# A message-passing layer on one core: pair work begins two slots later, ScalarE writes three seeds of the tail, GpSimd normalises one unit of the end

## The chip, the cores and the metric

The kernel runs on one core of a Trainium2 chip. The metric is the device time of one execution in microseconds; lower is better. The profile names the engines PE (TensorE matmul), PEld (TensorE weight load), DVE (VectorE), ACT (ScalarE), POOL (GpSimd) and SP (SyncE, which here only issues DMAs). Each engine works through its own instructions strictly in the order in which the program lists them, and waits on semaphores for the others.

## The reference

There are 6250 nodes and 100000 edges with 128 features each. Edges are sorted by `dst`; `src` is random.

```python
edge_index = jnp.stack([src, dst])          # row = src, col = dst
msg_in = concatenate([x[row], x[col], edge_attr], axis=-1)      # 100000 x 384
h = msg_in @ W + b                                               # W is 384 x 128
h = (h - mean(h)) * rsqrt(var(h) + 1e-5) * gamma + beta          # per edge
msg = relu(h)
out = segment_sum(msg, row, num_segments=6250)
x = x + out
result = (x - mean(x)) / sqrt(var(x) + 1e-5)                     # per node
```

## The kernel before

**Slots and scatters.** The edges are cut into 782 tiles of 128 edges, and four tiles make a slot, so the main loop runs over slots q = 0 to 195. In slot q, TensorE forms the part of `h` that comes from the edge features and from `x[dst]` (`edges`: eight matmul records of L619 and four of L623), ScalarE copies it from PSUM into a row buffer `hs` (`evict`: L633, and every third slot a `fill`, L568), and GpSimd scatters the rows, tile by tile, to an array in HBM that is ordered by source node (`scatters`: L650, one indirect DMA a tile). The row buffer is a ring of nine slots in three groups of three: `fill` waits until the three slots that last used its group have been scattered. From slot 13 to slot 194 each scatter of slot q-1 is also tied to a matmul of slot q (`TIE`, `add_manual_dep`), so GpSimd cannot run ahead of TensorE.

**Splits, pairs and steps.** The tiles form six splits of 168, 168, 168, 120, 80 and 78 tiles, each with its own array `sorted`. When a split has been scattered, its rows are read back in "pairs" (two blocks of 125 source nodes, `hl`, loaded by SP at L725, with four buffers). A pair goes through 14 to 16 steps (the list `FLOW`): VectorE builds one-hot matrices (`ones`, L748), TensorE transposes them (`turn`, L760), ScalarE copies the result (`turned`, L764) and writes the pair's rows into a PSUM bank (`seed`, L770), TensorE adds the source nodes' projections (`pick`, L787), ScalarE takes squares (`square`, L796) and roots, VectorE scales and clips (`scale`, L811), TensorE sums by node (`sums`, L820), VectorE adds to the accumulator (`add`, L826). A new pair enters every four steps. A pair of the first three splits has eight row blocks, of the fourth six; of the fifth split eight double pairs come first, then nine of four row blocks.

`work(n)` issues n steps; how many have to be issued by slot q is a straight line between the points of the list `due`, of which each is (slot, steps):

```python
n = steps_due(q + 1) - n_steps
work(min(n, 1))
evict(s, q)
...
work(n - 1)
if TIE[0] < q < TIE[1]:
    scatters(len(waiting) - PT, True)
```

In slot q these lines follow `edge_loads` and `edge_window` (up to four slots ahead, on SP), `edge_hot(q + 2)` (L607, VectorE) and `edges(s, q)`. The load of a pair is issued six steps before its `ones`. SP's queue holds edge loads (L141, L581, L593), clears of the next split's array (L236) and pair loads (L725) in one order; the first pair load of a split waits there until the split's last scatter has landed. The numbers of `due` before are (45, 0), (87, 100), (129, 200), (159, 300), (181, 400), (190, 432), (197, 468): the first three splits' pairs begin three slots behind the last slot of their split.

**The tail.** The pairs of the last split are the 14 units 0 to 13 (sizes 1, eleven times 2, 1, 1 pairs; four row blocks a pair). `tail(i)` issues for unit i: `root` and `scale` of unit i-1 (DVE, L898 and L905), `pick(0)` and `pick(1)` (PE), `ones` of unit i+2 (DVE, L854), `var` of unit i-3 (ACT, L947 and L950), `turn` of unit i+1 (PE, L864), `square` (ACT, L890 and L893), `turned` of unit i+1 (ACT, L867), `sums` and `add` of unit i-1 (PE L919, DVE L925), `begin` of unit i-1 (POOL, L932), `stats` of unit i-2 (DVE, L937), `norm` of unit i-3 (DVE, L956 and L958) and its `end`: two POOL instructions (L964, L965) and the store (SP, L970). In `pick` TensorE writes the rows into the bank by a product with the identity (L873), two records a time, and then adds twelve products (L879). The banks named `sel` are three, those named `hp` two; pair p of the last split takes `hp` where p mod 4 is 3.

The last four units are written out; a is the fourth last and b, c, d the last three. They end so:

```python
for u in (b, d, c):
    u.norm()
    u.end(True)
```

With `end(True)` VectorE normalises the unit's rows block by block (L968; four blocks for b, two for d and for c), and SP stores them (L970). The stores stand in SP's queue in the order b, d, c.

Of the kernel before, what the change touches and what calls it, by code (L numbers as in the profile page):

```python
# [17 lines left out]
D = 128  # L18
# [4 lines left out]
TILES = 782  # L23
LAST = E - (TILES - 1) * P
NB, BN = 50, 125
RUN = 8
NPAD = 6400
PT = 4
# [9 lines left out]
SPLITS = [(168, 4, 320, [12, 24, 44, 44, 44]),  # L38
          (168, 4, 320, [42, 42, 42, 42]),
          (168, 4, 320, [42, 42, 42, 42]),  # L40
          (120, 3, 192, [40, 40, 40]),
          (80, 2, 128, [40, 40]),
          (78, 2, 128, [39, 39])]
# [15 lines left out]
def first_tiles():  # L59
    out = [0]  # L60
    for n, _, _, _ in SPLITS:
        out.append(out[-1] + n)
    assert out[-1] == TILES
    return out
# [20 lines left out]
def fast_path(ctx, tc, io, bad_d, found):  # L85
# [3 lines left out]
    nc = tc.nc  # L89
    first_tile = first_tiles()  # L90
# [8 lines left out]
    def pe(i, cost=1):  # L99
        done.append((i.ins, cost))  # L100
        return i
# [76 lines left out]
    ident = const.tile([P, P], F32, name="ident")  # L178
# [551 lines left out]
    class Pairs:  # L730
# [35 lines left out]
        def seed(self, g):  # L766

            j0, m = self.groups[g]
            self.sel[g] = psum.tile([P, PT, P], F32, name="sel", bufs=BANKS["sel"])
            nc.scalar.copy(self.sel[g][:, :m, :], self.hl[:, j0:j0 + m, 0:D])  # L770

        def pick(self, g):


            j0, m = self.groups[g]
            if g in self.sel:
                sel = self.sel[g]
            else:
                name = "hp" if (g + self.p * len(self.groups)) % 2 else "sel"
                sel = psum.tile([P, PT, P], F32, name=name, bufs=BANKS[name])  # L780
                nc.tensor.matmul(sel[:, :m, :], ident, self.hl[:, j0:j0 + m, 0:D], start=True,
                                 stop=False, skip_group_check=True)
                self.sel[g] = sel
            for j in range(m):
                b = self.block(j0 + j)
                for i in range(3):
                    pe(nc.tensor.matmul(sel[:, j, :], self.ohn[:, j0 + j, :],  # L787
                                        xa[:, b, i * D:(i + 1) * D], start=False,
                                        stop=j == m - 1 and i == 2, skip_group_check=True))
# [45 lines left out]
    class Unit:  # L835
# [30 lines left out]
        def turned(self):  # L866
            nc.scalar.copy(self.ohn[:, :self.k, :], self.tr[:, :self.k, :])  # L867

        def pick(self, g):
            j0, m = g * self.kp, self.kp  # L870
            name = "hp" if (self.p0 + g) % 4 == 3 else "sel"
            sel = psum.tile([P, PT, P], F32, name=name, bufs=BANKS[name])
            nc.tensor.matmul(sel[:, :m, :], ident, self.hl[:, j0:j0 + m, 0:D], start=True,  # L873
                             stop=False, skip_group_check=True)
            self.sel[g] = sel
            for j in range(m):
                b = 2 * (self.p0 + g) + j % 2
                for i in range(3):
                    nc.tensor.matmul(sel[:, j, :], self.ohn[:, j0 + j, :],  # L879
                                     xa[:, b, i * D:(i + 1) * D], start=False,  # L880
                                     stop=j == m - 1 and i == 2, skip_group_check=True)
# [91 lines left out]
    n_split = len(SPLITS)  # L973
# [95 lines left out]
    TWINS = 8  # L1069
    pairs, first_item = [], []  # L1070
# [50 lines left out]
            n_steps += 1  # L1121

    LEAD, ENDQ, ENDS = 6, 1, 0
    LAG = 3
    MOST = 6.6

    due = []
    for s in range(1, n_split):
        q = first_tile[s] // PT + LAG
        if due:  # L1130
            q = max(q, due[-1][0] + int(NB * SPLITS[s - 2][1] / MOST))
        due.append((q, 4 * first_item[s - 1]))
    q, at0 = due[-1]
    due.append((q + int(4 * TWINS * SPLITS[-2][1] / MOST), at0 + 4 * TWINS))
    due.append((-(-TILES // PT) + ENDQ, len(pairs) * 4 + ENDS))

    def steps_due(q):
# [16 lines left out]
    for s, (n_tiles, _, _, _) in enumerate(SPLITS):  # L1154
        p0, p1 = first_tile[s] // PT, -(-first_tile[s + 1] // PT)
        slots = p1 - p0
        for i in range(slots):
            q = p0 + i
# [45 lines left out]
    def at(i):  # L1204
        return 0 <= i < n

    def tail(i):
        u = lambda j: units[i + j]
        if at(i - 1):
            u(-1).root()  # L1210
            u(-1).scale(0)
        if at(i):
            u(0).pick(0)
        if at(i - 1) and u(-1).n > 1:
            u(-1).scale(1)
        if at(i):
            if u(0).n > 1:
                u(0).pick(1)
        if at(i + 2):
            u(2).ones()  # L1220
            if at(i + 4):
                u(4).load()
        if at(i - 3):
            u(-3).var()
        if at(i + 1):
            u(1).turn()
        if at(i):
            u(0).square()
        if at(i + 1):
            u(1).turned()  # L1230
        if at(i - 1):
            for g in range(u(-1).n):
                u(-1).sums(g)
                u(-1).add(g)
            u(-1).begin(nc.gpsimd)
        if at(i - 2):
            u(-2).stats()
        if at(i - 3):
            u(-3).norm()
            u(-3).end()  # L1240
# [23 lines left out]
    for i in range(1, n - 1):  # L1264
        tail(i)
# [4 lines left out]
    a, b, c, d = units[-4:]  # L1270
# [21 lines left out]
    c.var()  # L1292
    for u in (b, d, c):
        u.norm()
        u.end(True)
    order.close()


@with_exitstack
def gnn_resnorm_kernel(ctx, tc, io):  # L1300
    nc = tc.nc
    keep = ctx.enter_context(tc.tile_pool(name="keep", bufs=1))
    bad_t = keep.tile([1, 1], I32, name="bad_t")
    with ExitStack() as inner:
        found = []
        fast_path(inner, tc, io, bad_t, found)
    with tc.If(found[0] > 0, preferred_fallthrough_block=True, label="general"):
        with ExitStack() as inner:
            general_path(inner, tc, io)
# [233 lines left out]
```

## Time and profile before

| what | value |
|---|---|
| median of 3 runs | 1121.99 us (1118.9 to 1122.06) |
| profiled execution | 1117.85 us |
| its span, first to last instruction | 1115.9 us |
| mean granted TensorE clock | 0.906 |
| busy: PE, DVE, ACT, POOL | 870.6, 846.7, 751.9, 795.9 us |

The profile's rows come from the profiled execution. Its span is 1.95 us shorter than its time. In a timeline row the first number is the start from the span's beginning, the second the duration, the bracket the idle time of the engine just before and what ended it.

### The profile page before, as it was taken

To read this page: it belongs to the slowest core of one execution; us is meant where nothing else is said; L and a number is where in the kernel's file an instruction comes from. 1 tells how busy PE (TensorE), PEld (TensorE's weight loads), DVE (VectorE), ACT (ScalarE), POOL (GpSimd) and SP (SyncE) were. 2 spreads that over 40 slices of the span, in tenths; PEclk is the share of its full clock that TensorE was granted. 3 is DMA by queue.
4 is the path that set the end of the run, shared out by engine and by line. 5 is a ranking of instruction groups with operands and counts; after the bars stand their busy time and mean duration, and the time that the engine had idled before them with its cause. 6 is when DMAs were issued, how large, how long until landed. Compare 5 with 4: busy or idle time off the path is not lost. (4 is left out here: it accounts for less than half of the span.)

```text
span 1115.9 us, 27253 instructions
## 1 busy us (share of the span) xinstructions
PE 870.6 (78%) x8886; PEld 805.4 (72%) x8886; DVE 846.7 (76%) x2368; ACT 751.9 (67%) x2980; POOL 795.9 (71%) x830
## 2 busy tenths in 40 slices
PE   6748755456878888598968678988989899987994
PEld 4647645456867887587868668888878788886773
DVE  8784556628769586688877668889898988877897
ACT  4324422126666667577777657898888899987895
POOL 2777777777777777777777777777777767774254
PEclk7879878668989788898989897999999999999998
DMA  7899999458777763877867648787778767844341
GB/s 216 262 267 272 283 311 284 150 182 286 230 228 253 234 205 126 270 231 245 274 223 242 186 134 281 244 253 241 230 245 259 226 209 241 262 136 141 105 134 61
DMA packets 128049, 247.19 MB, mean 222 GB/s; under 512 B 47005, under 2 KB 61231, under 8 KB 127897
## 3 DMA queue, kind: packets, MB, share of 16 engines
q1 hardware_dynamic: 101924, 191.92, 56.9%
q0 software_dynamic: 25104, 53.05, 13.2%
q8 instruction: 71, 1.16, 0.5%
q14 instruction: 80, 0.66, 0.2%
q10 hardware_dynamic: 870, 0.40, 0.1%
HBM read 155.49 MB, written 89.80 MB: 220 GB/s over the span
## 5 line engine op out<-in xcount | busy, mean ns | idle before, releaser
L650 POOL DMA_INDIRECT sorted<-hs,place_i x782 | 757.5, 969 | 249.8 <-issue 100.9
L787 PE MATMUL sel<-xa,ohn 128*128 128x128 bf16 x2550 | 188.9, 226 | 83.7 <-ACT sel L770 82.0
L619 PEld LDWEIGHTS hp<-w,eT 128*128 128x128 f32 x1564 | 216.4, 212 | 48.7 <-issue 30.2
L820 PE MATMUL pa<-msg,ohe 128*128 128x130 f32 x1700 | 236.6, 292 | 17.1 <-DVE acc L826 8.6
L619 PE MATMUL hp<-w,eT 128*128 128x128 f32 x1564 | 237.7, 300 | 14.1 <-ACT hs L633 14.1
L811 DVE SCALAR_TENSOR_TENSOR msg<-sel,rstd,cut 128x128 f32<-128x128 f32 x850 | 240.6, 345 | 8.0
L796 ACT ACTIVATE sq<-sel 128x128 f32<-128x128 f32 x850 | 223.7, 282 | 23.1 <-PE sel L787 23.1
L787 PEld LDWEIGHTS <-ohn 128*128 128x128 bf16 x2550 | 165.7, 101 | 94.3 <-issue 80.2
L820 PEld LDWEIGHTS pa<-msg,ohe 128*128 128x128 f32 x1700 | 213.9, 201 | 23.2 <-DVE acc L826 10.4
L796 ACT ACTIVATION_READ_ACCUMULATOR sq<-sel 128x1 f32 x850 | 180.9, 213 | 0.0
L748 DVE TENSOR_TENSOR ohe<-hl,beside 128x1024 f32<-128x1024 f32 (+2 forms) x117 | 130.2, 1113 | 57.2 <-DMA hl<-sorted 41.1
L633 ACT COPY hs<-hp 128x512 f32<-128x512 f32 x196 | 113.2, 579 | 59.1 <-PE hp L623 56.7
L770 ACT COPY sel<-hl 128x512 f32<-128x512 f32 (+1 forms) x225 | 128.1, 569 | 33.0 <-DVE msg L811 32.7
L764 ACT COPY ohn<-tr 128x1024 bf16<-128x1024 bf16 (+2 forms) x117 | 107.7, 921 | 5.3 <-PE tr L760 5.3
L607 DVE TENSOR_SCALAR ohd<-db,part_w 128x512 bf16<-128x512 bf16 x192 | 70.4, 367 | 51.7 <-DMA db<-drel_d 48.6
L568 ACT COPY hs<-sloc 128x12 f32<-128x12 f32 x66 | 14.1, 213 | 132.9 <-DMA sorted<-hs,place_i 131.1
L826 DVE TENSOR_TENSOR acc<-acc,pa 128x260 f32<-128x260 f32 x125 | 52.3, 418 | 57.6 <-PE pa L820 56.7
L760 PE MATMUL tr<-ident_h,ohe 128*128 128x128 bf16 x850 | 70.5, 227 | 26.8 <-DVE ohe L748 14.9
L623 PE MATMUL hp<-win,ohd 126*128 126x128 bf16 x782 | 80.8, 228 | 2.3 <-DMA win<-xb_d 2.3
L805 DVE RECIPROCAL rstd<-std 128x4 f32<-128x4 f32 (+1 forms) x225 | 38.1, 169 | 57.7 <-ACT std L799 56.0
L760 PEld LDWEIGHTS <-ohe 128*128 128x128 bf16 x850 | 55.6, 102 | 28.0 <-DVE ohe L748 16.1
L799 ACT ACTIVATE std<-ss,eps 128x4 f32<-128x4 f32 (+1 forms) x225 | 66.9, 297 | 7.3
(198 smaller groups left out, 1039.3 us busy)
## 6 DMA issues: line engine op xcount, KB each, us to landing
eT<-in_eT SPq DMA_DIRECT2D x96, 512.0 KB
hl<-sorted SPq DMA_DIRECT2D x75, 528.0 KB
db<-drel_d SPq DMA_DIRECT2D x96, 256.0 KB
sorted<-empty SPq DMA_DIRECT2D x100, 198.0 KB
hl<-sorted SPq DMA_DIRECT2D x50, 264.0 KB
sorted<-hs,place_i POOLq DMA_INDIRECT x782
hl<-sorted SPq DMA_DIRECT2D x25, 396.0 KB
sorted<-empty SPq DMA_DIRECT2D x50, 132.0 KB
```

Of the source, the lines that this page charges most:

```text
L619: pe(nc.tensor.matmul(hp[:, j, :], eT[:, at], w[:, 2, :], start=j == 0, stop=False, skip_group_check=True), 4)
L623: pe(nc.tensor.matmul(hp[:, j, :], oh[:3 * WN, at], win[:3 * WN, :], start=False, stop=j == m - 1, skip_group_check=True))
L633: nc.scalar.copy(hs[:, :m, 0:D], hp[:, :m, :])
L650: i = nc.gpsimd.indirect_dma_start(out=sorted_d[s][:, :], out_offset=bass.IndirectOffsetOnAxis(ap=place_i[:parts, t:t + 1], axis=0), in_=h ...
L748: nc.vector.tensor_tensor(self.ohe[:, :k, :], self.hl[:, :k, D:D + 1].to_broadcast([P, k, P]), row_bc(iota_p, k), op=ALU.is_equal)
L760: pe(nc.tensor.transpose(tr[:, j, :], half[:, j0 + j, 1::2], ident_h))
L764: nc.scalar.copy(self.ohn[:, :self.k, :], self.tr[:, :self.k, :])
L770: nc.scalar.copy(self.sel[g][:, :m, :], self.hl[:, j0:j0 + m, 0:D])
L787: pe(nc.tensor.matmul(sel[:, j, :], self.ohn[:, j0 + j, :], xa[:, b, i * D:(i + 1) * D], start=False, stop=j == m - 1 and i == 2, skip_gro ...
L796: nc.scalar.activation(sq[:, j, :], self.sel[g][:, j, :], AF.Square, accum_out=ss[:, j:j + 1])
L811: nc.vector.scalar_tensor_tensor(self.msg[:, j0 + j, 0:D], self.sel[g][:, j, :], rstd[:, j:j + 1], cut, op0=ALU.mult, op1=ALU.max)
L820: pe(nc.tensor.matmul(self.pa[:, h, :], self.ohe[:, i * k + j, :], self.msg[:, i * k + j, :], start=(j == h), stop=(j == k - 2 + h)), 4)
```

## The change

- `LAG` goes from 3 to 5 and `MOST` is gone. The points of `due` become (47, 0), (89, 100), (131, 200), (161, 300), (181, 400), (190, 432), (197, 468): the first four are two slots later, the last three as before. From slot 45 to slot 177 one to nine fewer steps have been issued than before by the end of the same slot (seven at slot 131, eight at slot 161); between slots 161 and 181 the steps come at 5.0 a slot, where they came at 4.55 from 159 to 181.
- In the tail's units 1 to 3 the rows of the second pair are written into their bank by ScalarE (a copy) and not by TensorE.
- Unit b is ended by POOL's two instructions, not by VectorE's four. `norm` of b stays on VectorE, and the three stores keep their order.

```diff
-        def pick(self, g):
+        def seed(self, g, engine):
             j0, m = g * self.kp, self.kp
             name = "hp" if (self.p0 + g) % 4 == 3 else "sel"
             sel = psum.tile([P, PT, P], F32, name=name, bufs=BANKS[name])
-            nc.tensor.matmul(sel[:, :m, :], ident, self.hl[:, j0:j0 + m, 0:D], start=True,
-                             stop=False, skip_group_check=True)
+            if engine is nc.scalar:
+                nc.scalar.copy(sel[:, :m, :], self.hl[:, j0:j0 + m, 0:D])
+            else:
+                nc.tensor.matmul(sel[:, :m, :], ident, self.hl[:, j0:j0 + m, 0:D], start=True,
+                                 stop=False, skip_group_check=True)
             self.sel[g] = sel
+
+        def pick(self, g, engine=None):
+            j0, m = g * self.kp, self.kp
+            self.seed(g, engine)
+            sel = self.sel[g]
             for j in range(m):
...
-    LAG = 3
-    MOST = 6.6
-
-    due = []
-    for s in range(1, n_split):
-        q = first_tile[s] // PT + LAG
-        if due:
-            q = max(q, due[-1][0] + int(NB * SPLITS[s - 2][1] / MOST))
-        due.append((q, 4 * first_item[s - 1]))
+    LAG = 5
+
+    due = [(first_tile[s] // PT + LAG, 4 * first_item[s - 1]) for s in range(1, n_split)]
     q, at0 = due[-1]
-    due.append((q + int(4 * TWINS * SPLITS[-2][1] / MOST), at0 + 4 * TWINS))
+    due.append((q + (TILES // PT + ENDQ - q) * 2 * TWINS // (NB // 2), at0 + 4 * TWINS))
     due.append((-(-TILES // PT) + ENDQ, len(pairs) * 4 + ENDS))
...
         if at(i):
             if u(0).n > 1:
-                u(0).pick(1)
+                u(0).pick(1, nc.scalar if i <= 3 else None)
...
     for u in (b, d, c):
         u.norm()
-        u.end(True)
+        u.end(u is not b)
```

## The prediction

> **What bounds the kernel now.** First the page: its rows of slices and its costliest group. GpSimd's row is flat at 7 from the second slice to the thirty-seventh.
>
> ```profile
> POOL 2777777777777777777777777777777767774254
> L650 POOL DMA_INDIRECT sorted<-hs,place_i x782 | 757.5, 969 | 249.8 <-issue 100.9
> ```
>
> 757.5 us busy and 249.8 us idle just before make 1007 us of the 1115.9 us span: the scatters fill everything but the tail. A flat 7 is an engine that does nothing else, since each scatter takes 0.97 us and the next comes 0.30 us later whatever happens. So I counted the scatters by stage (time, busy, count in brackets), and then read POOL's timeline for those that were later than that.
>
> ```profile
> 20.00:850.00 830.00, 630.65 (x651) 0.88 0.76 238
> 850.00:1012.00 162.00, 117.80 (x123) 1.00 0.70 213
> ...
> 659.27 0.97 POOL L650 DMA_INDIRECT sorted<-hs,place_i  x1 [0.30 <-issue]
> 853.95 0.97 POOL L650 DMA_INDIRECT sorted<-hs,place_i  x1 [1.26 <-PE pa L820]
> 876.12 0.97 POOL L650 DMA_INDIRECT sorted<-hs,place_i  x1 [0.86 <-PE pa L820]
> 886.42 0.96 POOL L650 DMA_INDIRECT sorted<-hs,place_i  x1 [1.47 <-PE pa L820]
> 901.09 0.97 POOL L650 DMA_INDIRECT sorted<-hs,place_i  x1 [0.79 <-ACT sel L770]
> 910.31 0.97 POOL L650 DMA_INDIRECT sorted<-hs,place_i  x1 [1.88 <-PE pa L820]
> 1008.63 0.97 POOL L650 DMA_INDIRECT sorted<-hs,place_i  x1 [1.83 <-PE pa L820]
> ```
>
> Up to 850 us a scatter comes every 830/651 = 1.275 us: nothing that the other engines do there shows in the end. From 850 to 1012 us it is 162/123 = 1.317 us, so about 123 x 0.042 = 5.2 us are lost; the six late rows hold 8.09 - 6 x 0.30 = 6.3 us. There GpSimd waits for TensorE (the tie to the products), so the other engines, "compute" from here on, set the pace. That is the most that can be won before the tail.
>
> How far compute is ahead is read by setting the copy of a slot beside that slot's first scatter (slots 131, 160 and 172).
>
> ```profile
> 659.31 0.59 ACT L633 COPY hs<-hp 128x512 f32<-128x512 f32 x1
> 688.62 0.97 POOL L650 DMA_INDIRECT sorted<-hs,place_i  x1 [0.30 <-DMA sorted<-hs,place_i]
> 825.86 0.59 ACT L633 COPY hs<-hp 128x512 f32<-128x512 f32 x1 [0.31 <-PE hp L623]
> 836.39 0.97 POOL L650 DMA_INDIRECT sorted<-hs,place_i  x1 [0.31 <-issue]
> 896.32 0.56 ACT L633 COPY hs<-hp 128x512 f32<-128x512 f32 x1
> ```
>
> The lead is 28.7 us at slot 131 (659.90 to 688.62), 9.9 at slot 160, 4.2 at slot 172 (to 901.09, above). So compute idles against the ring up to slot 131, and from there on it is slower than GpSimd until the lead is gone. What it loses after 660 us is what counts, and the largest loss is at the third split's end.
>
> ```profile
> SPq L725 <- DMA sorted<-hs,place_i: 70.5, 4, 30.0
> ...
> 664.17 0.34 SPq L725 DMA_DIRECT2D hl<-sorted  x1
> 668.27 1.22 DVE L748 TENSOR_TENSOR ohe<-hl,beside 128x1024 f32<-128x1024 f32 x1 [7.81 <-DMA hl<-sorted]
> 672.96 0.59 ACT L770 COPY sel<-hl 128x512 f32<-128x512 f32 x1 [10.74 <-DVE msg L811]
> 675.75 0.21 ACT L568 COPY hs<-sloc 128x12 f32<-128x12 f32 x1
> ```
>
> SP waits at the first pair load of each split for the last scatter (four times, 70.5 us). For the third it issues at 664.17, the rows land, and VectorE, which had stopped at `ones`, goes on at 668.27 after 7.81 us; ScalarE stood 10.74 us. The copy of slot 132 came only after that, at 675.9.
>
> **The delay of the pairs.** It removes and adds nothing: it issues the same steps later against the slots. Up to slot 131 (first two ends of splits) I put it at nothing: GpSimd's even pace covers it, with the lead of 28.7 us as cover; without that lead a later step would cost what it costs at the third end. At the third end, `ones` of the first pair (step 206) moves from slot 131 to slot 133. Before, compute stood from 660.46 to 668.27 with slot 131 copied and step 206 begun. After the change, `fill` of slot 132 needs the last scatter of slot 125, which is the very scatter that the load waits for, so both are free at about 664.1; then there are two copies and steps 204 and 205 to do while the rows land, about 4 us of ScalarE, and at 668.3 step 206 begins. The wait is not shorter: the same step starts at the same time. What is won is that slots 132 and 133 are done by then. A slot's own work is this:
>
> ```profile
> 681.70 1.11 PE L619 MATMUL hp<-w,eT 128*128 128x128 f32 x8
> 682.64 0.39 PE L623 MATMUL hp<-win,ohd 126*128 126x128 bf16 x4
> ...
> 676.00:820.00 144.00, 128.00 (x1486) 122.74 (x1486) 125.90 (x358) 125.35 (x515) 109.53 (x114) 0.98 0.77 243
> 834.00:928.00 94.00, 83.91 (x972) 79.58 (x972) 82.71 (x249) 85.46 (x356) 67.68 (x70) 1.00 0.77 236
> ```
>
> 1.5 us of TensorE, or 0.59 + 0.21/3 = 0.66 us of ScalarE. In these rows (busy PE, PEld, DVE, ACT, POOL) the first, third and fourth engine are all at 87 to 91%, so none of them alone is the bound and I take the middle, 1.1 us: two slots are **2.2 us** won, between 1.3 and 3.0. Compute arrives at slot 178 with the same steps issued as before (390), and from there the program is the same, so the gain reaches the tail by way of the tied scatters. The cover in between: at slot 161 eight more steps are outstanding, at 94 us / 77 steps = 1.2 us each 9.8 us; the lead pays for that, which should be about 9.9 + 9.8 + 2.2 = 22 us at slot 160, under the 28.7 that the ring has shown. SP's queue: the load passes two slots' edge loads and clears, which now go out ahead of the wait; no one waits longer for them. At the fourth end the load (slot 161) meets a scatter that is long issued, as now. The bounds: -6.3 us (no late scatter is left), and 0 if the steps alone, not the slots, set the pace.
>
> **The seeds.** TensorE loses three products with the identity, ScalarE gains three copies. What bounds that stretch is in the windows and in the waits of 1034 to 1051 us:
>
> ```profile
> 1034.00:1051.00 17.00, 16.58 (x158) 12.27 (x157) 13.86 (x42) 12.67 (x62) 2.46 (x3) 1.00 0.36 111
> 1051.00:1101.00 50.00, 48.31 (x455) 37.01 (x452) 48.34 (x208) 45.82 (x244) 30.05 (x30) 1.00 0.31 101
> ...
> 1040.42 1.08 PE L873 MATMUL sel<-hl,ident 128*128 128x512 f32 x2
> 1041.34 0.83 PE L879 MATMUL sel<-xa,ohn 128*128 128x128 bf16 x12
> ...
> 1040.62 0.28 ACT L890 ACTIVATE sq<-hp 128x128 f32<-128x128 f32 x1 [0.94 <-PE hp L879]
> 1042.21 0.28 ACT L890 ACTIVATE sq<-sel 128x128 f32<-128x128 f32 x1 [0.44 <-PE sel L879]
> 1045.23 0.40 ACT L947 ACTIVATE sq<-y,total 128x128 f32<-128x128 f32 x1 [0.65 <-DVE y L937]
> ```
>
> TensorE is full (16.58 of 17 us), ScalarE is not (12.67). A seed costs TensorE 0.92 us (1040.42 to 1041.34). ScalarE's copy of the same shape takes 0.59 us (L770, above) and stands just ahead of the waits of 0.94 and 0.65 us, which hide it; behind it in ScalarE's queue are only that unit's squares and, in unit 3, `var`. Without the cover it would cost its 0.59 us three times, 1.8. Walked through unit by unit: in units 1 and 2 (the rows are unit 2's, unit 1's are alike) the second pair's squares no longer wait 0.44 us, so ScalarE is 0.9 us early; VectorE's waits for the sums shrink with it; in unit 3 ScalarE's copy fills the 0.65 us, and its sixteen squares then run without a gap and become the limit. Unit 4's first product waits for ScalarE's transposed copy, 0.9 us earlier, and no longer for a seed, another 0.6. So **1.5 us** are won, between -0.3 (the copies uncovered, 1.8 less 1.5) and 2.8 (3 x 0.92). From 1051 us on TensorE and VectorE are both at 97%, and the lead is kept.
>
> **The end of unit b.** VectorE sheds four instructions, 1.11 us, and starts on d and c earlier; POOL gains two of 1.04 us, after a shift that is ready at 1107.6.
>
> ```profile
> 1104.80 1.04 POOL L965 TENSOR_TENSOR y<-y,shift 128x512 f32<-128x512 f32 x1
> 1107.45 0.16 DVE L958 SCALAR_TENSOR_TENSOR shift<-total,frstd 128x4 f32<-128x4 f32 x1
> 1107.65 1.11 DVE L968 TENSOR_SCALAR y<-y,frstd,shift 128x128 f32<-128x128 f32 x4
> 1108.56 0.29 ACT L950 ACTIVATE fstd<-var,eps 128x2 f32<-128x2 f32 x1
> 1110.05 0.60 DVE L968 TENSOR_SCALAR y<-y,frstd,shift 128x128 f32<-128x128 f32 x2
> 1110.68 0.33 SPq L970 DMA_DIRECT2D out<-y  x1
> ```
>
> c's root is ready at 1108.85, so VectorE would end c at about 1110.0 and not at 1110.65. But b's store is ahead of d's and c's in SP's queue: POOL ends b at 1107.65 + 2 x 1.04 + 0.07 = 1109.8, and three stores of 0.33 us, some 0.4 apart, put c's at 1109.85 + 0.8 = 1110.65, against 1110.68. **Nothing** is won. Upwards: if POOL stands while VectorE works on d and c, 4 x 0.28 = 1.1 us later. The Trainium skill has a rule against this edit: in "SBUF — State Buffer", section "Who interferes with whom", GpSimd's only port pair is one of VectorE's two, and a `tensor_scalar` in a two-port mode holds it, so that the other engine blocks until it is done. No L964 or L965 of this trace lies beside an L968, so no row shows it; by that rule the end would be up to 1.1 us later.
>
> **The sum.** -2.2 - 1.5 + 0 = -3.7 us: the profiled execution of 1117.85 us would become 1114.2. The median of the runs is 1121.99, 0.4% above that execution, and taken from it the time is **1118.3 us**.
>
> **The rivals.** (a) *Steps alone set the pace, or ScalarE's chain eats its copies:* gain 0 to 2, time about 1121. For it: TensorE's late products (L820) are the pairs', not the slots'. Against: ScalarE and TensorE at 87 to 91%. (b) *GpSimd never starves again and the tail keeps all of TensorE's time:* 6.3 + 2.8 = 9.1, time 1112.9. For it: the lead of 22 us at slot 161. Against: the same steps must be done by slot 178. (c) *The denser stretch costs more than the lead holds, and it gets slower:* between slots 161 and 181 steps come at 5.0 a slot. Their place is the six-block pairs at 820 to 930 us, where GpSimd already waits for L820. If the ring stops compute at 664 to 820 us and the lead at slot 161 stays under 15 us, some 5 of the 9.8 us of postponed steps come back as late scatters, time about 1127. For it: a scatter is tied to products, and there are now more products of pairs to each slot. Against: the 28.7 us that the ring has held. (d) *The delay does not do what it says:* the ring holds slots 132 and 133 back as the load did, and only the seeds act: gain 1.5, time 1120.5. Against: one scatter frees both.
>
> **How the numbers follow.** The runs of before lie 0.28% apart, so 0.3%, 3.4 us, is what a measurement of this kernel can tell. The forecast, gain 2 to 6, has 0.48 (0.38 of it over 3.4 us); (a) 0.10; (b) 0.12; (c) 0.23; (d) 0.07. Faster 0.38 + 0.12 = 0.50, same 0.10 + 0.10 + 0.07 = 0.27, slower 0.23. The range goes from (b) less half the runs' spread of 3.2 us, 1111, to just short of (c), 1126.5, which leaves out half of (c) and little else; the forecast's own is 1116 to 1120.
>
> **What would show it.** Right: VectorE's wait for `hl` at the third end under 3 us; the copies of slots 132 and 133 before 669 us; a lead near 22 us at slot 160; fewer late scatters between 850 and 920 us; TensorE's twelve products of unit 4 some 1.5 us closer to the last scatter; c's store where it is. Wrong: a scatter rate from 850 to 1012 us slower than 1.317 us, or units 1 to 3 no shorter.

## The result, and the profile after

| | before | after |
|---|---|---|
| median of 8 runs each, same chip | 1120.66 us (1118.9 to 1122.35) | 1116.87 us (1114.62 to 1118.29) |
| profiled execution | 1117.85 us | 1118.29 us |
| its span | 1115.9 us | 1116.5 us |
| mean granted TensorE clock | 0.906 | 0.904 |

The ratio is 0.9964, with a 95% interval of 0.9953 to 0.9976: the changed kernel is 3.8 us faster (2.7 to 5.3). The profiled execution of after is its slowest run. It was late before the change touches anything: the scatter behind the third split's end, which is the first scatter of the fourth split, starts at 666.11 us, where it started at 663.08 before.

```profile
663.08 0.97 POOL L650 DMA_INDIRECT sorted<-hs,place_i  x1 [0.31 <-DMA sorted<-hs,place_i]
666.11 0.96 POOL L650 DMA_INDIRECT sorted<-hs,place_i  x1 [0.31 <-ACT sel L770]
```

Most of those 3.03 us come from three scatters at 32, 48 and 90 us, where no step had been moved yet. So the traces are compared by stages, each counted from its own start, and not by their spans. From the tail's `pick` on, line numbers are higher after the change, by 8 for most of the tail: the root L893 is L901.

**The third split's end.** First a wait of after over the whole span, then its timelines of SP, ScalarE and VectorE around 668 us.

```profile
SPq L725 <- DMA sorted<-hs,place_i: 47.4, 4, 17.8
```

```profile
668.09 0.34 SPq L725 DMA_DIRECT2D hl<-sorted  x1
668.06 0.21 ACT L568 COPY hs<-sloc 128x12 f32<-128x12 f32 x1 [0.79 <-DMA sorted<-hs,place_i]
668.17 0.58 ACT L633 COPY hs<-hp 128x512 f32<-128x512 f32 x1
671.51 0.59 ACT L633 COPY hs<-hp 128x512 f32<-128x512 f32 x1
671.70 1.22 DVE L748 TENSOR_TENSOR ohe<-hl,beside 128x1024 f32<-128x1024 f32 x1 [1.60 <-DMA hl<-sorted]
```

Over the four ends SP's wait went from 70.5 to 47.4 us. At this end VectorE stands 1.60 us before its `ones` (before: 7.81). ScalarE's `fill` goes on at 668.06, SP issues the load at 668.09, and at 668.17 ScalarE copies slot 132: one scatter frees the ring and the load together, as forecast. The copies of slots 132 and 133 are done at 668.75 and 672.10, about when `ones` begins (671.70). Before, slot 132 came 7.6 us behind it. Counted from the scatter behind the split's end, `ones` itself begins 0.40 us later than before (5.59 against 5.19), and its load is issued 0.89 us later (1.98 against 1.09).

**The lead and the late scatters.** ScalarE's copy of slot 160 and that slot's first scatter, POOL in one stage (time, busy, count), and POOL's rows from 850 to 1012 us whose wait was over 0.9 us, all of after:

```profile
817.89 0.56 ACT L633 COPY hs<-hp 128x512 f32<-128x512 f32 x1
839.24 0.96 POOL L650 DMA_INDIRECT sorted<-hs,place_i  x1 [0.30 <-ACT ohn L764]
```

```profile
850.00:1012.00 162.00, 119.26 (x124) 1.00 0.66 210
```

```profile
908.41 0.97 POOL L650 DMA_INDIRECT sorted<-hs,place_i  x1 [1.92 <-PE pa L820]
...
1005.57 0.97 POOL L650 DMA_INDIRECT sorted<-hs,place_i  x1 [0.96 <-ACT sq L796]
1010.08 0.97 POOL L650 DMA_INDIRECT sorted<-hs,place_i  x1 [2.28 <-PE pa L820]
```

The lead at slot 160 is 839.24 - 818.45 = 20.8 us, where it was 9.9. From 850 to 908 us no scatter waits over 0.5 us any more; before, four did. From 850 us on a scatter comes every 162/124 = 1.306 us (before 1.317, with one scatter fewer). Counted from the first scatter of the fourth split, the copy of slot 178 ends 2.3 us earlier than before (262.31 against 264.63). That is not yet a gain: ahead of this copy ScalarE has done 95 copies of `turned` (L764, 0.78 us) before and 94 after the change, so one step is still to come. Ahead of the copy of slot 179 it is 96 in both. Here are those two copies, of before and then of after:

```profile
931.33 0.59 ACT L633 COPY hs<-hp 128x512 f32<-128x512 f32 x1
932.74 0.59 ACT L633 COPY hs<-hp 128x512 f32<-128x512 f32 x1
```

Counted as above, it ends 1.6 us earlier (267.22 against 268.84), and the last scatter ends 1.6 us earlier too (359.16 against 360.73). At the first two ends nothing was won: from the 61st scatter to the last of the third split it is 564.56 us, where it was 564.06.

**The seeds.** The window of after over the tail's beginning (busy PE, PEld, DVE, ACT, POOL, then granted clock), and the roots of units 0 to 4 and 13, of before and then of after:

```profile
1034.00:1051.00 17.00, 16.09 (x169) 12.82 (x167) 14.93 (x50) 15.94 (x79) 3.25 (x4) 1.00 0.40 130
```

```profile
1033.60 0.30 ACT L893 ACTIVATE std<-ss,eps 128x4 f32<-128x4 f32 x1
1038.49 0.30 ACT L893 ACTIVATE std<-ss,eps 128x8 f32<-128x8 f32 x1
1043.38 0.30 ACT L893 ACTIVATE std<-ss,eps 128x8 f32<-128x8 f32 x1
1048.79 0.30 ACT L893 ACTIVATE std<-ss,eps 128x8 f32<-128x8 f32 x1
1054.70 0.30 ACT L893 ACTIVATE std<-ss,eps 128x8 f32<-128x8 f32 x1
...
1100.90 0.30 ACT L893 ACTIVATE std<-ss,eps 128x4 f32<-128x4 f32 x1
```

```profile
1034.98 0.30 ACT L901 ACTIVATE std<-ss,eps 128x4 f32<-128x4 f32 x1
1039.32 0.30 ACT L901 ACTIVATE std<-ss,eps 128x8 f32<-128x8 f32 x1
1043.67 0.30 ACT L901 ACTIVATE std<-ss,eps 128x8 f32<-128x8 f32 x1
1048.59 0.30 ACT L901 ACTIVATE std<-ss,eps 128x8 f32<-128x8 f32 x1
1053.87 0.30 ACT L901 ACTIVATE std<-ss,eps 128x8 f32<-128x8 f32 x1
...
1100.13 0.30 ACT L901 ACTIVATE std<-ss,eps 128x4 f32<-128x4 f32 x1
```

Root to root, the units took 4.89, 4.89, 5.41, 5.91 us before and take 4.34, 4.35, 4.92, 5.28 after; from unit 0 to unit 13 it was 67.30 us and is 65.15, **2.15 us** less. The first twelve products of unit 4 stand 24.58 us behind the end of the last scatter, where they stood 26.75 us behind it. ScalarE's busy time in the window rose from 12.67 to 15.94 of 17 us: its copies filled its gaps.

**The end.** VectorE's timeline of after, then POOL's and the last store of SP's:

```profile
1106.69 0.17 DVE L966 SCALAR_TENSOR_TENSOR shift<-total,frstd 128x4 f32<-128x4 f32 x1
1107.23 0.56 DVE L966 SCALAR_TENSOR_TENSOR shift<-total,frstd 128x2 f32<-128x2 f32 x1
1107.83 1.40 DVE L976 TENSOR_SCALAR y<-y,frstd,shift 128x128 f32<-128x128 f32 x2
1109.60 0.60 DVE L976 TENSOR_SCALAR y<-y,frstd,shift 128x128 f32<-128x128 f32 x2
```

```profile
1106.73 1.04 POOL L972 TENSOR_TENSOR y<-y,frstd 128x512 f32<-128x512 f32 x1 [1.66 <-DVE frstd L964]
1107.85 1.04 POOL L973 TENSOR_TENSOR y<-y,shift 128x512 f32<-128x512 f32 x1
1110.23 0.33 SPq L978 DMA_DIRECT2D out<-y  x1
```

VectorE's second shift takes 0.56 us where the first takes 0.17, and d's two blocks take 1.40 us where c's take 0.60: each ends with the POOL instruction beside it (1107.77 and, for the first of d's blocks, 1108.89). From b's shift to c's store it is 3.54 us (1106.69 to 1110.23); before it was 3.23 (1107.45 to 1110.68). And what follows c's store became longer too. From unit 13's root to the end of the span it was 15.05 us and is 16.35: **1.3 us** lost.

### The profile page after: what moved, and what is told of

It is laid out like the page before. It is cut to its first block, busy times and chain, and to the rows that moved or that the text cites. A ratio compares the mean times of both kernels' runs of the same rounds, so it can differ in the third digit from the quotient of the medians.

```text
span 1116.5 us, 27245 instructions
## 1 busy us (share of the span) xinstructions
PE 868.9 (78%) x8880; PEld 805.1 (72%) x8880; DVE 846.0 (76%) x2364; ACT 754.6 (68%) x2983; POOL 798.5 (72%) x832
## 5 line engine op out<-in xcount | busy, mean ns | idle before, releaser
L619 PE MATMUL hp<-w,eT 128*128 128x128 f32 x1564 | 240.5, 303 | 22.0 <-ACT hs L633 22.0
L619 PEld LDWEIGHTS hp<-w,eT 128*128 128x128 f32 x1564 | 218.7, 214 | 53.0 <-issue 27.2
L820 PE MATMUL pa<-msg,ohe 128*128 128x130 f32 x1700 | 231.3, 288 | 15.3 <-DVE acc L826 8.6
L820 PEld LDWEIGHTS pa<-msg,ohe 128*128 128x128 f32 x1700 | 210.8, 199 | 20.2 <-DVE acc L826 10.2
L764 ACT COPY ohn<-tr 128x1024 bf16<-128x1024 bf16 (+2 forms) x117 | 107.8, 921 | 5.3 <-PE tr L760 5.3
L623 PEld LDWEIGHTS <-ohd 126*128 126x128 bf16 x782 | 66.2, 105 | 5.1 <-issue 1.4
```

Source lines behind the costliest of these rows:

```text
L619: pe(nc.tensor.matmul(hp[:, j, :], eT[:, at], w[:, 2, :], start=j == 0, stop=False, skip_group_check=True), 4)
L623: pe(nc.tensor.matmul(hp[:, j, :], oh[:3 * WN, at], win[:3 * WN, :], start=False, stop=j == m - 1, skip_group_check=True))
L820: pe(nc.tensor.matmul(self.pa[:, h, :], self.ohe[:, i * k + j, :], self.msg[:, i * k + j, :], start=(j == h), stop=(j == k - 2 + h)), 4)
```

## The experiments

The experiments ran on chips on which the kernel before takes about 1353 us, and each is compared with it there. On those chips TensorE's stream has gaps that no row explains, as the timeline of TensorE in the first experiment (the delay alone) shows:

```profile
616.62 0.22 PE L760 MATMUL tr<-ident_h,ohe 128*128 128x128 bf16 x1
617.98 0.22 PE L760 MATMUL tr<-ident_h,ohe 128*128 128x128 bf16 x1 [1.14 <-issue]
619.39 0.27 PE L760 MATMUL tr<-ident_h,ohe 128*128 128x128 bf16 x2 [1.19 <-issue]
...
```

Transposes that should follow each other come one or a few at a time, over 1 us apart, and nothing that the trace shows held them. There are some 200 such gaps over 0.25 us in a trace, 167 to 214 us together; on the first chip there was one. The traces of these chips also put some 450 to 540 us of waits of the engines down to releasers that they can't name, those of the first chip none, so whether TensorE stops by itself or waits for something that isn't recorded is open. In either case GpSimd waits for TensorE nearly everywhere and compute has little lead; here slot 160's copy and first scatter, in the same kernel:

```profile
1005.51 0.58 ACT L633 COPY hs<-hp 128x512 f32<-128x512 f32 x1 [1.35 <-PE tr L760]
1013.96 0.96 POOL L650 DMA_INDIRECT sorted<-hs,place_i  x1 [1.58 <-ACT hs L633]
```

That is 7.9 us, against 20.8 on the first chip. At the ends of splits there is next to no wait for rows: SP's pair loads wait for scatters at most 5.5 us in all, in any of these traces, and the first `ones` behind the third end starts at least 13 us after its load was issued. What the delay takes away on the first chip does not exist on these, so they can weigh the tail but not the delay's mechanism.

### The delay alone

```diff
-                u(0).pick(1, nc.scalar if i <= 3 else None)
+                u(0).pick(1)
...
-        u.end(u is not b)
+        u.end(True)
```

> Only the pairs' delay (LAG 5); the tail as before. Theory (slots 132 and 133 are done inside the wait for the third split's rows): 1.3 to 3.0 us faster than before, and the last scatter, counted from the first scatter of split 1, that much earlier. Rival (the steps alone set the pace, or the denser stretch from slot 161 to 181 gives it back): 0 to 1 us, or slower by up to 5.

Measured: 1350.0 against 1352.94 us, ratio 0.9976 (0.9955 to 0.9998). A second time:

> The delay alone once more. If compute is far ahead of GpSimd at the third end, as in the profile of before (lead of 28 us): 1.3 to 3.0 us faster than before. If TensorE's stream stops by itself all along, as in the runs so far beside this one (lead of 5 us throughout, late scatters everywhere), no wait for the third split's rows is there to be hidden: no change within 2 us.

Measured: 1351.58 against 1352.82 us, ratio 0.9989 (0.9969 to 1.0009). The medians say a gain of 1 to 3 us, and the intervals reach from a loss of 1 to a gain of 6. As the wait it is meant to shorten isn't there, this does not show the mechanism; nor does it bear on rival (c), whose price depends on a lead that isn't there either.

### The seeds alone

The list `due` and the end as before; only `pick(1, nc.scalar if i <= 3 else None)` is left of the change.

> Only ScalarE's three seeds, the delay and the end of unit b as before. Theory: the unit roots of the tail, counted from the last scatter's end, come 2.2 us earlier from unit 4 on (the changed kernel's trace shows this; the prediction said 1.5), and the time is 1.5 to 2.2 us shorter. Rival (ScalarE is late by its copies): 0 to 0.5 us.

Measured: 1349.65 against 1352.94 us, ratio 0.9979 (0.996 to 0.9999), a gain of 2.8 us (0.1 to 5.4). The trace is sharper than the time. The roots of units 0, 1 and 13 there:

```profile
1273.54 0.30 ACT L901 ACTIVATE std<-ss,eps 128x4 f32<-128x4 f32 x1
1277.88 0.30 ACT L901 ACTIVATE std<-ss,eps 128x8 f32<-128x8 f32 x1
...
1338.70 0.30 ACT L901 ACTIVATE std<-ss,eps 128x4 f32<-128x4 f32 x1
```

Units 1 and 2 take 4.34 us each, and it is 65.16 us from unit 0 to 13, against 67.31 in the delay alone on the same chips: 2.15 us, the same as on the first chip. From unit 0's root on there is no scatter to be tied to, and the units agree between the chips within 0.02 us; that is why their gains can be added. Ahead of that root they do not agree: from the end of the last scatter to it there are 9.7 and 9.8 us on the first chip and 13.8 to 17.8 on these.

### The end alone

`due` and `pick(1)` as before; only `u.end(u is not b)` is left of the change.

> Only unit b ended by GpSimd. The prediction: no change. Theory after the changed kernel's trace (VectorE's two-block normalisation of unit d stands behind GpSimd's instruction, and GpSimd's closing sequence of 6.8 us after its last instruction now ends last): 0.8 to 1.4 us slower than before, the span from b's shift to the end 9.8 us instead of 8.45. Rival (chance of that one execution): within 0.3 us, 8.45 us.

Measured: 1355.01 against 1352.94 us, ratio 1.0022 (1.0003 to 1.0041): slower by 0.4 to 5.5 us. From unit 13's root to the end of the span it is 16.21 us; with VectorE ending b it is 14.98 to 15.17 in twelve traces, of before and of the other experiments. So POOL's end costs 1.1 us here and 1.3 us in the changed kernel. VectorE and POOL at the end of this kernel:

```profile
1342.86 0.56 DVE L966 SCALAR_TENSOR_TENSOR shift<-total,frstd 128x2 f32<-128x2 f32 x1
1343.46 1.40 DVE L976 TENSOR_SCALAR y<-y,frstd,shift 128x128 f32<-128x128 f32 x2
```

```profile
1342.36 1.04 POOL L972 TENSOR_TENSOR y<-y,frstd 128x512 f32<-128x512 f32 x1 [1.66 <-DVE frstd L964]
1343.48 1.04 POOL L973 TENSOR_TENSOR y<-y,shift 128x512 f32<-128x512 f32 x1
```

The same 0.56 and 1.40 us as in the changed kernel, beside the same two POOL instructions, with neither delay nor seeds. The Trainium skill ("SBUF — State Buffer", "Who interferes with whom") says that where VectorE and GpSimd contend, the one that issues first has the shared ports for its whole instruction and the other waits until it is done; the rows agree, with POOL as the holder and VectorE as the one that waits.

### The change without its end

```diff
-        u.end(u is not b)
+        u.end(True)
```

> The changed kernel with VectorE ending unit b again. If GpSimd's end of b costs about 1.3 us: 1.3 us faster than the changed kernel, about 5 us faster than before (ratio 0.9953). If it costs nothing, as predicted: 3.8 us faster than before (ratio 0.9964).

Measured: 1349.35 against 1352.94 us, ratio 0.9968 (0.9947 to 0.999). Twice more:

> Delay and seeds, unit b ended by VectorE, once more beside the others. Theory: 2 (delay) + 2.2 (seeds) = 4.2 to 5 us faster than before, with the last unit's root 2.2 us closer to the last scatter and 15.0 us from there to the end. Rival (the end of b is free): 3.8 us, as the changed kernel.

> Delay and seeds without GpSimd's end of b. With the lead at the ring's limit: 5 us faster than before (delay 2.9, seeds 2.2). With a lead of 5 us: 2.2 to 3 us faster, the seeds alone.

Measured: 1349.21 us, 0.9966 (0.9945 to 0.9986), and 1348.55 us, 0.9967 (0.9942 to 0.9993). Three times 4.3 to 4.6 us faster than before. Unit 0 to 13 takes 65.15 to 65.17 us, unit 13 to the end 14.98 to 15.07: the seeds' gain and the old end. Less the seeds' 2.15 us, some 2.3 us are left for the delay, more than the third expectation gave it with so short a lead. By what they would be won on these chips is not known, and the intervals, over 2 us to either side, allow nothing as well. The changed kernel itself was not run on these chips, so that this version beats it is read from the stages: 16.35 - 15.0 = 1.3 us.

### Which end of a split the delay wins at

First only the third and fourth ends two slots later, then only the first two, both with neither seeds nor POOL's end:

```diff
-    due = [(first_tile[s] // PT + LAG, 4 * first_item[s - 1]) for s in range(1, n_split)]
+    due = [(first_tile[s] // PT + (LAG if s > 2 else 3), 4 * first_item[s - 1])
+           for s in range(1, n_split)]
```

> The delay only at the third and fourth ends of splits: points (45, 0), (87, 100), (131, 200), (161, 300), the tail as before. Theory (only the third end matters): all of the delay's gain, 1.3 to 3.0 us faster than before, VectorE's wait for the third split's rows under 3 us. Rival (the first two ends carry the gain): no change.

```diff
+    due = [(first_tile[s] // PT + (3 if s in (3, 4) else 5), 4 * first_item[s - 1])
+           for s in range(1, n_split)]
```

> The delay only at the first two ends: points (47, 0), (89, 100), (129, 200), (159, 300), the tail as before. Theory (GpSimd's even pace covers both ends): no change, within 1 us, and the wait of about 7.8 us at the third end is there again. Rival: 1.3 to 3.0 us faster.

Measured: 1351.34 against 1354.07 us, ratio 1.0 (0.9977 to 1.0022), for the late ends, and 1351.92 us, 1.0001 (0.9982 to 1.0019), for the first two. Neither is told from no change, nor from the delay's whole effect on these chips. With little lead and no wait for rows, the test had nothing to tell apart; it is inconclusive. For the first two ends the first chip's traces answer it (564.56 against 564.06 us, above): nothing was won there.

### A longer delay

From the delay alone, `LAG = 8`, with the fifth split's point left at 5:

```diff
-    LAG = 5
+    LAG = 8
...
-    due = [(first_tile[s] // PT + LAG, 4 * first_item[s - 1]) for s in range(1, n_split)]
+    due = [(first_tile[s] // PT + (5 if s == 5 else LAG), 4 * first_item[s - 1])
+           for s in range(1, n_split)]
```

> The first four points eight slots behind: (50, 0), (92, 100), (134, 200), (164, 300), (181, 400), the tail as before. Theory (two slots are enough to hide the third split's wait, and more delay leaves steps undone while the ring holds compute): some 8 more steps of 1.2 us are still to do at slot 134 and come back as late scatters, 4 to 9 us slower than with five slots, 2 to 7 us slower than before. Rival (each slot of delay wins a slot's own work): 2 to 4 us faster than five slots behind.

> The first four points eight slots behind, once more. With the lead at the ring's limit: 2 to 7 us slower than before, 4 to 9 slower than five slots behind. With a lead of 5 us throughout: no change within 2 us.

Measured: 0.9994 (0.998 to 1.0008) and 1.0003 (0.998 to 1.0026). No gain, and no loss over 0.3% either; the loss of 2 to 7 us did not come. It does not decide how the first chip would take it, where the lead that pays for postponed steps was 20.8 us.

### ScalarE seeds the second pair of every unit

From the change without its end:

```diff
-                u(0).pick(1, nc.scalar if i <= 3 else None)
+                u(0).pick(1, nc.scalar)
```

> As the run before it, but ScalarE seeds the second pair of every unit from 1 to 11. From 1051 us on ScalarE was busy 45.8 of 50 us; a copy of 0.59 us to each 5.4 us unit makes it the bound at about 5.6 us. Theory: the tail from unit 0's root to unit 13's takes 65.15 + 8 x 0.2 = 66.8 us, 0 to 2.5 us longer than with three seeds. Rival (TensorE alone is the bound): 0.15 us a unit shorter, down to VectorE's 5.25, 64.0 us.

Measured in one run: 1350.6 us. Unit 0 to 13 takes 65.86 us, 0.7 more than with three seeds. The roots of units 4 and 5, and the window of 1284 to 1330 us in this kernel and, second, in the first run of the change without its end:

```profile
1287.20 0.30 ACT L901 ACTIVATE std<-ss,eps 128x8 f32<-128x8 f32 x1
1292.89 0.30 ACT L901 ACTIVATE std<-ss,eps 128x8 f32<-128x8 f32 x1
```

```profile
1284.00:1330.00 46.00, 38.27 (x403) 31.50 (x400) 44.32 (x184) 45.45 (x233) 26.93 (x26) 1.00 0.31 104
```

```profile
1284.00:1330.00 46.00, 45.89 (x437) 34.98 (x435) 44.90 (x188) 43.67 (x227) 26.29 (x25) 1.00 0.31 104
```

TensorE is relieved, from 45.89 to 38.27 us, and ScalarE is full (45.45 of 46): a unit takes 5.69 us, where it took 5.47. From unit 3 on ScalarE has `var` in each unit as well, so a copy there is on the path. So the cover that the prediction named (waits of 0.94 and 0.65 us) is not there in the later units, and in the traces three seeds did better than none and than eleven.

## Why the prediction was right, and where it was not

Forecast were -3.7 us for the whole; the medians give -3.8 (-2.7 to -5.3). In part that is luck. From the scatter behind the third end on, the two traces give 1.6 + 2.15 - 1.3 = 2.45 us, and of the three terms none has its forecast size: the delay and the end brought less, the seeds more.

**The delay: right in the mechanism, as far as it can be seen.** A wait of VectorE under 3 us was forecast and 1.60 measured; a lead near 22 us at slot 160, and it is 20.8; fewer late scatters from 850 to 920 us, and there is none before 908. Both late copies were to be done before 669 us. They end at 668.75 and 672.10 in a trace that is 3.03 us late at that point, so that by the clock of before the second ends at 669.07, 0.07 us past the mark. Rival (d) falls with the copies beside the load. As to the size, 2.2 us were forecast by slot 178, and the two traces say 1.6, at slot 179 and at the last scatter alike. Of the 0.6 us that are missing, 0.40 may be those by which `ones` starts later, as it was to start at the same time as before; no run shows it by itself. From slot 179 on nothing is given back, so rival (c) does not show. The medians, less the tail's two terms, give the delay more, 3.8 - 2.15 + 1.3 = 2.9 us (1.8 to 4.4, by the interval of the ratio), so its size is not settled between the two. Both speak against the part of rival (a) by which the delay wins nothing. All this rests on the first chip's traces and times; no experiment could test the delay's mechanism.

**The seeds: right in the mechanism, short in the size.** 1.5 us were forecast and 2.15 measured, alone and together with the rest. The gain was to be complete at unit 4's first products, and it is: they come 2.17 us closer to the last scatter. Of the 1.5 us, 0.9 were to come from units 1 and 2, which brought 0.55 + 0.54 = 1.09. The mis-sized term is the other, "another 0.6" behind unit 3's seed: units 3 and 4 are shorter by 0.49 + 0.63 = 1.12. In all it is 0.72 us for each of the three products of 0.92 us taken off a full TensorE; ScalarE's 0.59 us were covered, as the 5.69 us units without cover show by contrast.

**The end of unit b: the step that failed.** Forecast was "nothing", with +1.1 us as the upper bound; it cost 1.1 and 1.3. b's store did go out about when it was forecast, 2.23 us behind b's shift where 2.40 were forecast. Two things were missed. First, the bound had POOL stand while VectorE works. It is VectorE that stands, so d and c, which are behind in its queue, were late: c's store waited for VectorE's last block and not for b's store, and it is 3.54 us from b's shift to c's store instead of 3.23, 0.3 lost. The profile before already had a row of VectorE held up by POOL, a little earlier in the same tail:

```profile
1103.05 0.68 POOL L932 TENSOR_TENSOR y<-acc,g 128x256 f32<-128x256 f32 x1 [1.02 <-DVE acc L925]
1103.31 0.44 DVE L958 SCALAR_TENSOR_TENSOR shift<-total,frstd 128x4 f32<-128x4 f32 x1
```

This shift takes 0.44 us and ends with POOL's instruction (1103.75 and 1103.73); b's own shift, with no POOL instruction beside it, takes 0.16. Second, the prediction ended its sum at the last store. Behind it every engine closes, that is, goes through the instructions that end the program, and POOL's closing is long. Here are three groups of these instructions in after, two of POOL's queue and one of SP's (ns at least, median, at most; first and last start), and behind them POOL's drains in before:

```profile
L1541 POOLq DRAIN  x3: 40/113/3426, 1112.2 to 1116.2; - x3
L1309 POOLq INC_SWDGE_SEM  x1: 1017/1017/1017, 1111.2 to 1111.2; - x1
L1541 SPq DRAIN  x3: 7/7/13, 1114.9 to 1115.9; - x3
```

```profile
L1539 POOLq DRAIN  x3: 40/113/3426, 1108.9 to 1115.7; - x3
```

In before the long drain of 3.43 us began at 1108.9, 3.1 us after POOL's last instruction, and was over at 1112.35, before SP's closing. In the changed kernel POOL's last instruction ends at 1108.89 and the drain goes from 1112.22 to 1115.65. SP has two of its drains behind it at 1115.02 (in before at 1115.14), and its third, at the very end, comes 0.27 us behind POOL's long one. So POOL closes last, and that adds about 0.7 us to the 0.3. The remaining 0.3 lie between c's store and SP's drains, 4.46 us in before and 4.79 in after. That stretch is 4.39 us in the first run of the change without its end and 4.57 in the end alone, so it is not shown that the change made it longer.

## What to carry to other kernels

A gain that moves work between engines holds only where the taker has gaps in that very unit: read the waits unit by unit, as three seeds won 2.15 us and eleven won 1.44. In the last microseconds count every engine to the end of its closing, not to the last store: an instruction given to an engine that was long done can make that engine the last. Where a step waits for a transfer, putting independent work ahead of it can win most of that work's time even if the wait's end doesn't move.

## What the runs showed that was not expected

- A GpSimd operation on a 128x512 block held up some of VectorE's instructions beside it until it ended: a shift of 0.16 us took 0.56, a block of 0.33 us took 1.15, in both kernels in which POOL ends b. Others were not held up: the four of L945 beside POOL's L972 at 1102.92 us take 0.34 us each, as elsewhere.
- GpSimd's closing takes 6.8 us from the end of its last instruction (1108.89 to 1115.65; 6.5 in before), 3.43 of it in one drain.
- On some chips TensorE's stream has some 200 gaps of 0.26 to 12 us with no releaser in the trace, 167 to 214 us in all, and the kernel takes 1353 us and not 1121; the tail's units are the same to 0.02 us, and no such gap stands in the last 90 us. Why is open: no run here tells.
